# A three-stage decoder on one core: masks and maxima per head on VectorE, heads added from PSUM, layernorm's step on ScalarE, new plan costs

## The chip, the core and the metric

The kernel runs on one core of one Trainium2 chip. A core has TensorE (PE) for matrix products, VectorE (DVE), ScalarE (ACT), GpSimd (POOL), and SyncE (SP), which issues the DMAs. Each engine takes its instructions in order from its own queue; engines wait for each other by semaphores. TensorE writes its results to PSUM, of which this kernel uses eight banks of 128 x 512 float32[...]. The metric is the device time in microseconds of one execution.

## What is computed

There are 32 batch entries of 128 tokens with 128 features, in float32. Three stages follow each other, each with a residual sum and a layernorm:

```python
x = layernorm(x + attn(x, W))               # 16 heads of width 8, q = k = y; values are the whole x
x = layernorm(x + xattn(x, ctx, ctx, ...))  # 16 heads of width 8, band mask |i-j| <= 64
x = layernorm(x + ffn(x, ...))              # two layers, below
```

In the first stage each head's output is `attn @ x` (128 x 128), and the 16 heads are joined by one weight matrix of 2048 x 128. A layer of the third stage is

```python
h = shift_token(x); q, k, v = split(h @ wqkv)          # 8 heads of width 64
q = l2norm(q) * qs; k = l2norm(k) * ksc; q, k = rotary_xpos(q, k)
sim = (8 * q) @ k.T; sim[(i < j) | (i > j + 64)] = -max; x = x + (softmax(sim) @ v) @ wo
h = layernorm(shift_token(x)) * lg + lb; a, g = split(h @ w1 + b1)
x = x + (a * gelu(g)) @ w2 + b2
```

## The kernel before

**Order of the work.** The 32 entries are cut into ten groups (SIZES, one to four entries). A list of generator steps, sorted by due times made from LAGS, CLOSE and SPREAD, interleaves four stages of different groups: self_attention, cross_attention, and layer 0 and layer 1. The steps do not issue instructions; they record operations in a `Plan`, each with an engine, a cost in ns, the values it reads and writes, and flags. `Plan.issue` then simulates the five engines with these costs and fixes the order on each engine: it takes the operation that can start first, among those at most AHEAD operations beyond the first undone one. The same step hands out buffers from rings, PSUM banks (`m`, eight), large SBUF tiles (`big`) and small ones, some of which (KEEP) are held back for the oldest value that waits. So costs and constants decide the order of instructions, and with it who waits for whom.

**Self attention** (`self_half`, one call for each half of eight heads of an entry, 64 calls). TensorE makes x W_h for four heads at a time (L579, 128x512), which ScalarE copies to `zs` (L586). Scores come from a split into bf16 parts (L542). VectorE takes the maxima of each bank of four heads (L421, in `maxima`), GpSimd splits them in two bf16 parts (L435, L436), TensorE turns them and subtracts them in PSUM (L442, L452), and ScalarE takes exponentials of a whole bank (L600). TensorE multiplies by `zs`, which has a column of ones for the sums (L608), into three banks of three, three and two heads. VectorE takes reciprocals (L617) and multiplies a whole bank into `zs` (L618). GpSimd adds the eight heads in three steps, 4, 2 and 1 wide (L628), and adds the result to the residual `x0` (L632).

**Cross attention** (`cross_batch`, 32 calls of two halves). The band mask is a matmul of an identity with a bf16 mask, 128x512, into each bank (L539), and the scores accumulate on it. VectorE takes the maxima, ScalarE one exponential per head with the negated maximum as bias (L466, in `exps_of`), TensorE turns the result (L481, in `turned_half`), VectorE copies it (L488) and TensorE multiplies by the values (L724).

**Local attention** (`local_batch`, 64 calls). TensorE makes q, k and v (L796) and ScalarE copies them (L801). ScalarE squares q and k (L807), VectorE sums the squares (L810), GpSimd raises the sums to the power -1/2 (L813, L814). The rotary step is a product with the swapped halves on GpSimd (L824) and three VectorE steps over q and k together, 128x1024: product with the cosines (L833), sum (L837), product with the norms (L840). Eight transposes (L851) and copies (L857), then scores of 64-row matmuls on top of the mask matmuls (L865, L871), maxima and exponentials with row sums (L421, L466), division (L885, L886), transposes, output and projection (L900, L912), residual (L919).

**Layernorm** (`layernorm`): statistics on VectorE (L382, L389), the power on GpSimd (L397 to L400), and scale and shift by one VectorE instruction per entry (L407).

VectorE and GpSimd steps marked `port=True` are booked as sharing a port.

Of the kernel before, what the change touches and what calls it, by code (L numbers as in the profile page):

```python
# [28 lines left out]
AHEAD = 430  # L29
LAGS = (0, 1.35, 2.75, 4.1)  # L30
RINGS = (23, 16, 6, 4)
KEEP = (2, 3, 5)
NEAR = 0
EARLY = (0, 0.2)
CLOSE = (0.9, 0.85, 0.9, 1, 1, 1, 1.2, 1.05, 0.85, 0.95)
SPREAD = (1.4, 1.0, 0.7, 1.5)
LH, LD = 8, 64
INNER = LH * LD
# [38 lines left out]
class Plan:  # L77

# [51 lines left out]
    def issue(self, ahead, near=80.0, hop=60.0, table_ns=1300.0, tiling_ns=160.0, dma_ns=1800.0):  # L132
# [13 lines left out]
        def time_of(k):  # L146
            e = ops[k][0]
            return max([0.0] + [end[d] + (hop if ops[d][0] != e else 0.0) for d in ops[k][3]])
# [5 lines left out]
        shared = 0.0  # L154
# [5 lines left out]
        while len(order) < n:  # L160
            best = None
            for e in engines:
                choice, least = [], None
                for k, t in ready[e]:
                    if k > first + ahead:
                        continue
                    start = max(clock[e], t, shared if ops[k][7] else 0.0)
# [5 lines left out]
                    for vs in need.values():  # L173
# [4 lines left out]
                        start = max(start, sorted(q.free)[len(vs) - 1][0] + hop)  # L178
# [4 lines left out]
                    if e == "PE" and ops[k][8][0] != state:  # L183
                        start += tiling_ns
# [19 lines left out]
            if e == "SP":  # L204
                line = max(line, s + dma_ns) + ns
                end[k], clock[e] = line + 400.0, s + 450.0
            else:
                end[k] = clock[e] = s + ns
            if tab:
                table[e] = tab  # L210
            if port:
                shared = end[k]
# [19 lines left out]
def decoder_kernel(ctx: ExitStack, tc: tile.TileContext, a: dict, out: bass.AP):  # L232
# [109 lines left out]
    def prepare_cross():  # L342
# [3 lines left out]
               cols[:, 0:1], cols[:, 0:1], SCALE, 1.0, ALU.mult, ALU.mult), [], [w_cross])  # L346
# [15 lines left out]
    def turned(src, n):  # L362

        tp, t = Val(mring), Val(mid)
        op("PE", 113 * n, turn(src, tp, n), [src], [tp], hold=[t])
        op("ACT", 140 + 113 * n,
# [10 lines left out]
    def layernorm(src, dst, n):  # L377
# [6 lines left out]
        op("DVE", n * 290, stats, [src], [st])  # L384
# [6 lines left out]
        op("DVE", n * 175, aggr, [st], [mv])  # L391
# [10 lines left out]
        op("POOL", 1100 + 260 * n, rest, [], [mv])  # L402

        def apply():
            x, y = group(src.t), group(dst.t)
            for j in range(n):
                nc.vector.tensor_scalar(  # L407
                    y[:, j, :], x[:, j, :], mv.t[:, 8 + j : 9 + j], mv.t[:, 12 + j : 13 + j],
                    ALU.mult, ALU.add,
                )  # L410

        op("DVE", 200 * n, apply, [mv] + ([src] if src is not dst else []), [dst])
# [4 lines left out]
    def maxima(s, nm):  # L417
        for b in range(2):
            op(
                "DVE", 690,  # L420
# [5 lines left out]
    def minus_max(s):  # L426
# [6 lines left out]
        def parts():  # L433
# [4 lines left out]
        op("POOL", 440, parts, [nm], [hl])  # L438
        mp = Val(mring, lambda t: t[:, 0:64].bitcast(BF16))
        op(  # L440
            "PE", 110,
# [4 lines left out]
        op("ACT", 260, lambda: nc.scalar.copy(mT.t, mp.t), [mp], [mT])  # L446
        return mT

    def emit_max(s, mT):
        for b in range(2):  # L450
            for i in range(4):
# [3 lines left out]
                )  # L455

    def exps_of(s, sums=None):
# [4 lines left out]
        for b in range(2):  # L462
# [8 lines left out]
            op("ACT", 4 * (345 if sums else 255) + 60, exps, [s[b], (nm, b)],  # L471
# [3 lines left out]
    def turned_half(e, et, b, eng, src):  # L475
# [9 lines left out]
        op("PE", 4 * 113, pe, [src], [tp], hold=[et])  # L485
        copy = nc.vector.tensor_copy if eng == "DVE" else nc.scalar.copy
        op(eng, 690 if eng == "DVE" else 590,
# [6 lines left out]
    def in_slots(src, n, keep_src, moving):  # L494
# [4 lines left out]
        op("ACT", 140 + 113 * n,  # L499
           lambda: nc.scalar.copy(pv.t[:, 0, every], src.t[:, every]), [src], [(pv, 0)])  # L500
        op("POOL", 316 * n,
# [3 lines left out]
        op("ACT", 140 + 113 * n,  # L505
           lambda: nc.scalar.copy(pv.t[:, 1, every], rest.t[:, every]), [rest], [(pv, 1)])
        op("POOL", 316 * n,
# [26 lines left out]
    def scores_of(s, stationary, moving, hh, window=False):  # L534
# [12 lines left out]
        op("PE", 8 * 62 + 432 * window, pe,  # L547
# [22 lines left out]
    def self_half(j, hh, x0, xT, ys):  # L570
# [3 lines left out]
        for b in range(2):  # L574
# [3 lines left out]
                "PE", 875,  # L578
# [6 lines left out]
                "ACT", 590,  # L585
# [10 lines left out]
        op("PE", 8 * 60, lambda: emit_max(s, mT), [mT, (w_self, 2)], s)  # L596
        e = Val(big, heads)
        for b in range(2):
            op("ACT", 590,
# [3 lines left out]
        for k, (h0, n) in enumerate(((0, 3), (3, 3), (6, 2))):  # L603
# [9 lines left out]
            op("PE", 230 * n, pe, [e] + [(zs, i) for i in range(3)], [oz])  # L613
            rl = Val(small)

            def scale(oz=oz, rl=rl, h0=h0, n=n):
                nc.vector.reciprocal(rl.t[:, 0:n], oz.t[:, 0:n, D])  # L617
                nc.vector.tensor_tensor(  # L618
                    zs.t[:, h0 : h0 + n, 0:D], oz.t[:, 0:n, 0:D],
                    rl.t[:, 0:n].unsqueeze(2).to_broadcast([P, n, D]), ALU.mult,  # L620
                )

            op("DVE", 175 + 30 + 133 * n, scale, [oz], [rl, (zs, ("o", k))])

        z = lambda h0, n: zs.t[:, h0 : h0 + n, 0:D]
        for n, ns in ((4, 1270), (2, 730), (1, 450)):
            op("POOL", ns,
# [495 lines left out]
```

## Time and profile before

Three runs took 1293.61, 1292.23 and 1289.26 us; the median is 1292.23. The profiled execution took 1292.12 us, with a span of 1290.3 us between its first and last instruction and a granted TensorE clock of 0.987.

| Line | Engine, operation | Count | Busy us |
|---|---|---|---|
| L466 | ACT exponentials of the masked stages | 1024 | 323.0, and 115.9 for 512 accumulator reads |
| L421 | DVE maxima | 384 | 245.6 |
| L813 | POOL power | 64 | 200.8 |
| L628, L632 | POOL additions of heads | 256 | 163.2 and 31.8 |
| L618, L617 | DVE scaling of heads, reciprocals | 192, 192 | 98.7, 32.4 |
| L833, L840, L837 | DVE rotary and norms | 64 each | 86.0, 87.2, 80.5 |
| L407 | DVE layernorm's step | 160 | 72.3 |
| L539, L865 | PE mask matmuls | 128, 128 | 48.7, 39.1 |

How to read the profile: the page has busy time of each engine, the span in 40 equal slices with the busy share in tenths, the chain of work that ended last (followed back from the last instruction to what released each step), and groups of instructions by line with their busy time, the mean length of one, and the idle time of the engine before them with what ended it. `big<-m,sm` names the tiles written and read, without buffer numbers. The timeline lists instructions by start. Busy time is a union: where an instruction begins before its predecessor's recorded end, the overlap counts once. Ends of matmuls are modelled.

### The profile page before, as it was taken

What the parts mean: (1) busy time and instruction counts of PE and PEld (TensorE: products, weight loads), DVE (VectorE), ACT (ScalarE), POOL (GpSimd) and SP (SyncE); (2) the same over time, 40 slices, a digit from 0 to 9 for tenths busy, and PEclk for the clock granted to TensorE, in tenths of its full rate; (3) what the DMA queues carried; (4) which work ended last, traced back from release to release, by engine and by line L of the source; (5) the groups of instructions that cost most, each with busy time, mean ns of one, the idle gap of its engine ahead of it and who ended that gap; (6) DMA issues with size and microseconds to landing.
All of it is one profiled execution on the core that took longest, in us unless ns stands there. A gap on an engine that the chain in (4) does not pass through costs nothing.

```text
span 1290.3 us, 27579 instructions
## 1 busy us (share of the span) xinstructions
PE 1213.9 (94%) x9730; PEld 888.0 (69%) x9730; DVE 1070.3 (83%) x2134; ACT 966.2 (75%) x2762; POOL 835.3 (65%) x1094
## 2 busy tenths in 40 slices
PE   7988999999979999999999999999999989999996
PEld 4766677776767865777777667778667657567664
DVE  2677889878968888887798889979899999988786
ACT  4564777777867778777778778858889968879863
POOL 2866657765857389555687468653966963786454
PEclk9999999999989999999999999999999989999999
DMA  9886414240154420732005401330300000000000
GB/s 254 209 213 193 124 39 105 56 128 9 37 136 109 99 56 1 174 89 65 20 25 138 124 1 34 94 95 18 97 2 12 18 18 2 9 1 2 2 1 25
DMA packets 173930, 91.44 MB, mean 71 GB/s; under 512 B 155872, under 2 KB 161888, under 8 KB 173536
## 3 DMA queue, kind: packets, MB, share of 16 engines
q1 hardware_dynamic: 173792, 89.67, 27.5%
q8 instruction: 77, 1.26, 0.4%
q14 instruction: 61, 0.50, 0.1%
HBM read 49.79 MB, written 39.85 MB: 69 GB/s over the span
## 4 chain that ended last, share of the span: by engine, by line
PE 45%; POOL 15%; DVE 14%; ACT 6%; issue 3%; DMA 1%; SPq 0%; POOLq 0%; DVEq 0%; ACTq 0%
PE m L796 6%; POOL sm L813 6%; PE m L481 5%; PE m L944 4%; PE m L608 4%; ACT big L466 3%; PE m L900 3%; PE m L579 3%; PE m L871 3%; PE m L912 3%; POOL big L824 3%; PE m L964 3%; PE m L724 2%; DVE sm L421 2%; PE m L542 2%
## 5 line engine op out<-in xcount | busy, mean ns | idle before, releaser
L466 ACT ACTIVATE big<-m,sm 128x128 f32<-128x128 f32 x1024 | 323.0, 399 | 54.5 <-DVE sm L421 53.9
L421 DVE TENSOR_REDUCE sm<-m 128x4 f32<-128x512 f32 x384 | 245.6, 681 | 45.4 <-PE m L871 21.5
L813 POOL TENSOR_TENSOR sm<-sm,nhalf 128x16 f32<-128x16 f32 x64 | 200.8, 3137 | 36.8 <-DVE sm L810 26.7
L628 POOL TENSOR_TENSOR big<-big 128x512 f32<-128x512 f32 (+2 forms) x192 | 163.2, 850 | 83.8 <-DVE big L618 36.8
L824 POOL TENSOR_TENSOR big<-big,layer_w 128x512 f32<-128x512 f32 x128 | 162.4, 1269 | 76.4 <-ACT big L801 71.1
L796 PE MATMUL m<-layer_w,mid 128*128 128x512 f32 x384 | 193.2, 612 | 4.2 <-DVE xb L971 2.1
L481 PE MATMUL m<-ident,big 128*128 128x128 f32 x1024 | 144.4, 276 | 15.4 <-DVE big L886 9.6
L481 PEld LDWEIGHTS m<-ident,big 128*128 128x128 f32 x1024 | 115.7, 141 | 54.9 <-issue 21.9
L579 PE MATMUL m<-self_w,mid 128*128 128x512 f32 x256 | 131.1, 626 | 7.0 <-DMA self_w<-in_self_w 5.7
L608 PEld LDWEIGHTS m<-big,big 128*128 128x128 f32 x1024 | 123.0, 191 | 13.7 <-issue 7.5
L608 PE MATMUL m<-big,big 128*128 128x129 f32 x1024 | 129.9, 276 | 0.9 <-DVE big L618 0.3
L466 ACT ACTIVATION_READ_ACCUMULATOR big<-m,sm 128x1 f32 x512 | 115.9, 226 | 0.0
L586 ACT COPY big<-m 128x512 f32<-128x512 f32 x128 | 75.1, 600 | 38.8 <-PE m L579 38.0
L618 DVE TENSOR_TENSOR big<-m,sm 128x384 f32<-128x384 f32 (+1 forms) x192 | 98.6, 514 | 6.6
L886 DVE TENSOR_TENSOR big<-big,sm 128x512 f32<-128x512 f32 x128 | 98.2, 767 | 4.6 <-DMA slots<-big 0.2
L542 PEld LDWEIGHTS <-big 72*128 72x128 bf16 x1024 | 72.3, 98 | 41.3 <-issue 20.2
L542 PE MATMUL m<-big,big 72*128 72x128 bf16 x1024 | 87.8, 220 | 9.6 <-DMA big<-slots 8.9
L488 ACT COPY big<-m 128x512 f32<-128x512 f32 x128 | 75.0, 598 | 28.3 <-PE m L481 19.4
L796 PEld LDWEIGHTS m<-layer_w,mid 128*128 128x128 f32 x384 | 64.7, 193 | 42.6 <-issue 27.9
L857 ACT COPY big<-m 128x512 f32<-128x512 f32 x128 | 71.6, 608 | 29.7 <-PE m L851 29.1
L944 PE MATMUL m<-mid,layer_w 128*128 128x512 f32 (+7 forms) x240 | 89.5, 516 | 2.7 <-DVE mid L935 1.5
L488 DVE COPY big<-m 128x512 f32<-128x512 f32 x128 | 82.0, 681 | 11.5 <-PE m L481 10.7
(116 smaller groups left out, 2611.4 us busy)
## 6 DMA issues: line engine op xcount, KB each, us to landing
slots<-big SPq DMA_DIRECT2D x384, 96.0 KB
big<-slots SPq DMA_DIRECT2D x128, 288.0 KB
layer_w<-in_layer_w SPq DMA_DIRECT2D x2, 1877.0 KB
mid<-in_xt SPq DMA_DIRECT2D x5, 256.0 KB
mid<-in_xg SPq DMA_DIRECT2D x5, 256.0 KB
mid<-in_ct SPq DMA_DIRECT2D x5, 256.0 KB
out<-xb SPq DMA_DIRECT2D x5, 256.0 KB
self_w<-in_self_w SPq DMA_DIRECT2D x2, 512.0 KB
```

The lines of the kernel that those rows point to most:

```text
L421: lambda b=b: nc.vector.tensor_reduce(nm.t[:, 4 * b : 4 * b + 4], s[b].t, AX.X, ALU.max, negate=True),
L466: nc.scalar.activation(e.t[:, h, :], s[b].t[:, h - 4 * b, :], AF.Exp, bias=nm.t[:, h : h + 1], accum_out=sums.t[:, h : h + 1] if sums else ...
L481: nc.tensor.transpose(tp.t[:, 128 * c : 128 * c + 128], e.t[:, 4 * b + c, :], ident)
L488: lambda: copy(et.t[:, 4 * b : 4 * b + 4, :], tp.t.rearrange("p (c k) -> p c k", c=4)),
L542: nc.tensor.matmul(s[b].t[:, i, :], st[:, h, :], mv[:, h, :], start=not window and i == 0, stop=i == 3,)
L579: lambda zp=zp, h0=h0: nc.tensor.matmul(zp.t, group(xT.t)[:, j, :], attn_w[:, h0 : h0 + 4, :], start=True, stop=True),
L608: nc.tensor.matmul(oz.t[:, i, :], e.t[:, h0 + i, :], zs.t[:, h0 + i, :], start=True, stop=True,)
L628: lambda n=n: nc.gpsimd.tensor_tensor(z(0, n), z(0, n), z(n, n), ALU.add),
L796: lambda hp=hp, i=i: nc.tensor.matmul(hp.t, group(hT.t)[:, j, :], wqkv[l][:, INNER * i : INNER * (i + 1)], start=True, stop=True),
L813: nc.gpsimd.tensor_tensor(rn.t[:, 0:16], rn.t[:, 0:16], nhalf, ALU.pow)
L824: nc.gpsimd.tensor_tensor(r2.t[:, :, :, d0 : d0 + 32], q[:, :, :, d1 : d1 + 32], tabs[l][:, :, d0 : d0 + 32].unsqueeze(2).to_broadcast([P, ...
L944: lambda t=t, off=off, c0=c0, m=m: nc.tensor.matmul(t.t[:m, every], w1[l][:, off + c0 : off + c0 + m], hT.t[:, every], start=True, stop=True),
```

## The change

1. The heads of self attention are no longer written back to `zs` and added by GpSimd. After the reciprocals, VectorE runs one scalar-tensor-tensor instruction per head: x0's entry = PSUM head times its reciprocal, plus x0's entry. L618, L628 and L632 go.
2. The band masks are no longer matmuls. The tables maskw and maskl are negated, and q (through SCALE and the rotary tables) is negated too, so that the scores arrive negated. One VectorE instruction per head adds the mask, multiplies by a scale, writes the masked negated score to SBUF, and gives its minimum as an accumulator output. The exponential then reads SBUF, in place, with scale -1.
3. In local attention that scale is q's norm, per row and head, so q's own norm step goes. The cosine products read PSUM directly, q and k apart, and the sums and k's norm are 128x512 steps. The transposes of q can begin when q's part is there.
4. Layernorm's step moves to ScalarE, one activation per entry with scale and bias.
5. The plan: all costs of operations are new, an engine's tail and hop times replace one hop time, the port's booking is per engine, and AHEAD, LAGS, RINGS, KEEP, NEAR, CLOSE and SPREAD have new values.

The diff, cut to its core (the changed costs of untouched operations are left out):

```diff
-AHEAD = 430
-LAGS = (0, 1.35, 2.75, 4.1)
-RINGS = (23, 16, 6, 4)
-KEEP = (2, 3, 5)
-NEAR = 0
+AHEAD = 290
+LAGS = (0, 1.55, 2.75, 4.1)
+RINGS = (23, 17, 6, 4)
+KEEP = (2, 2, 5)
+NEAR = 60
...
-CLOSE = (0.9, 0.85, 0.9, 1, 1, 1, 1.2, 1.05, 0.85, 0.95)
-SPREAD = (1.4, 1.0, 0.7, 1.5)
+CLOSE = (0.9, 0.85, 0.9, 1, 1, 1, 1.15, 0.95, 0.85, 0.95)
+SPREAD = (1.3, 1.0, 0.7, 1.5)
...
+TTR = 215
...
+    TAIL = {"PE": 165.0, "DVE": 82.0, "ACT": 115.0, "POOL": -75.0, "SP": 0.0}
+    HOP = {"PE": 55.0, "DVE": 32.0, "ACT": 36.0, "POOL": 77.0, "SP": 25.0}
...
-                nc.vector.tensor_scalar(
-                    y[:, j, :], x[:, j, :], mv.t[:, 8 + j : 9 + j], mv.t[:, 12 + j : 13 + j],
-                    ALU.mult, ALU.add,
+                nc.scalar.activation(
+                    y[:, j, :], x[:, j, :], AF.Identity,
+                    scale=mv.t[:, 8 + j : 9 + j], bias=mv.t[:, 12 + j : 13 + j],
                 )
-        op("DVE", 200 * n, apply, [mv] + ([src] if src is not dst else []), [dst])
+        op("ACT", 365 * n, apply, [mv] + ([src] if src is not dst else []), [dst])
...
+    def masked_exps(s, mask, scale=lambda h: 1.0, sums=None, extra=()):
+        nm = Val(small)
+        e = Val(big, heads)
+        for b in range(2):
+            def masked(b=b):
+                for h in range(4 * b, 4 * b + 4):
+                    nc.vector.tensor_tensor_reduce(
+                        out=e.t[:, h, :], in0=s[b].t[:, h - 4 * b, :], in1=mask,
+                        scale=scale(h), scalar=-MASKED, op0=ALU.add, op1=ALU.min,
+                        accum_out=nm.t[:, h : h + 1],
+                    )
+            op("DVE", TTR * 4, masked, [s[b], (w_self, 2), *extra], [(e, b), (nm, b)])
+            def exps(b=b):
+                for h in range(4 * b, 4 * b + 4):
+                    nc.scalar.activation(
+                        e.t[:, h, :], e.t[:, h, :], AF.Exp, bias=nm.t[:, h : h + 1], scale=-1.0,
+                        accum_out=sums.t[:, h : h + 1] if sums else None,
+                    )
+            op("ACT", 1384 if sums else 1004, exps, [(nm, b)],
+               [(e, b)] + ([(sums, b)] if sums else []), table="exp")
+        return e
...
             def scale(oz=oz, rl=rl, n=n):
+                y = group(x0.t)[:, j, :]
                 nc.vector.reciprocal(rl.t[:, 0:n], oz.t[:, 0:n, D])
-                nc.vector.tensor_tensor(
-                    zs.t[:, h0 : h0 + n, 0:D], oz.t[:, 0:n, 0:D],
-                    rl.t[:, 0:n].unsqueeze(2).to_broadcast([P, n, D]), ALU.mult,
-                )
+                for i in range(n):
+                    nc.vector.scalar_tensor_tensor(
+                        y, oz.t[:, i, 0:D], rl.t[:, i : i + 1], y, ALU.mult, ALU.add
+                    )
-        z = lambda h0, n: zs.t[:, h0 : h0 + n, 0:D]
-        for n, ns in ((4, 1270), (2, 730), (1, 450)):
-            op("POOL", ns,
-               lambda n=n: nc.gpsimd.tensor_tensor(z(0, n), z(0, n), z(n, n), ALU.add),
-               [], [zs], port=n > 1)
-        y = lambda: group(x0.t)[:, j, :]
-        op("POOL", 450,
-           lambda: nc.gpsimd.tensor_tensor(y(), y(), z(0, 1)[:, 0, :], ALU.add),
-           [zs], [(x0, j)])
+            op("DVE", 100 + 205 * n, scale, [oz], [rl, (x0, j)])
...
-            scores_of(s, qs, ks, hh, True)
-            e = exps_of(s)
+            scores_of(s, qs, ks, hh)
+            e = masked_exps(s, maskw[:, 0:P])
...
+            if i < 2:
+                op("DVE", 620,
+                   lambda hp=hp, i=i: nc.vector.tensor_tensor(
+                       qr.t[:, i], hp.t.rearrange("p (h d) -> p h d", d=LD),
+                       tabc[l][:, i].unsqueeze(1).to_broadcast([P, LH, LD]), ALU.mult),
+                   [hp, w_layer[l]], [(qr, i)])
...
+        for i in range(2):
+            op("DVE", 610,
+               lambda i=i: nc.vector.tensor_tensor(qr.t[:, i], qr.t[:, i], r2.t[:, i], ALU.add),
+               [r2], [(qr, i)], port=True)
+        op("POOL", 3171, power, [], [rn])
+        op("DVE", 610,
+           lambda: nc.vector.tensor_tensor(
+               qr.t[:, 1], qr.t[:, 1],
+               rn.t[:, 8:16].unsqueeze(2).to_broadcast([P, LH, LD]), ALU.mult),
+           [rn], [(qr, 1)], port=True)
...
-            for b in range(2):
-                nc.tensor.matmul(
-                    s[b].t, identb, maskl, start=True, stop=False
-                )
...
-        e = exps_of(s, rl)
+        norm = lambda h: rn.t[:, 2 * (h % 4) + h // 4 : 2 * (h % 4) + h // 4 + 1]
+        e = masked_exps(s, maskl[:, 0:P], norm, rl, [rn])
```

## The prediction

> **What bounds the kernel now.** I read the page first: busy time by engine, the slices, the chain that ended last.
>
> ```profile
> PE 1213.9 (94%) x9730; PEld 888.0 (69%) x9730; DVE 1070.3 (83%) x2134; ACT 966.2 (75%) x2762; POOL 835.3 (65%) x1094
> ...
> PE   7988999999979999999999999999999989999996
> ...
> DVE  2677889878968888887798889979899999988786
> ACT  4564777777867778777778778858889968879863
> POOL 2866657765857389555687468653966963786454
> ...
> PE 45%; POOL 15%; DVE 14%; ACT 6%; issue 3%; DMA 1%; SPq 0%; POOLq 0%; DVEq 0%; ACTq 0%
> ```
>
> TensorE is full in nearly every slice; the chain stays longest on it. Busy time over stretches of the span confirms it for the long middle (columns PE, PEld, DVE, ACT, POOL):
>
> ```profile
> 0.00:35.00 35.00, 27.42 (x118) 15.00 (x119) 9.88 (x22) 17.79 (x34) 7.92 (x39) 1.00 0.92 262
> ...
> 130.00:1150.00 1020.00, 978.44 (x7961) 719.74 (x7959) 878.93 (x1718) 795.64 (x2295) 683.86 (x831) 0.99 0.25 61
> ```
>
> In the middle TensorE fills 978.4 of 1020 us, 96%, beside a VectorE at 86%. VectorE is thus second, with about 10% to spare. In the first 35 us it has hardly any work (9.9 us): its first reduction starts at 26.5 us.
>
> Then the groups by shape, for the price of each edited line (busy us, mean ns of one):
>
> ```profile
> L421 DVE TENSOR_REDUCE sm<-m 128x4 f32<-128x512 f32 x384 | 245.6, 681 | 45.4 <-PE m L871 21.5 <-PE m L542 18.3 <-ACT big L600 4.2
> ...
> L618 DVE TENSOR_TENSOR big<-m,sm 128x384 f32<-128x384 f32 x128 | 71.5, 558 | 4.4
> ...
> L539 PE MATMUL m<-masks,identb 128*128 128x512 bf16 x128 | 48.7, 381 | 1.2 <-DVE big L618 1.1
> ...
> L407 DVE TENSOR_SCALAR mid<-mid,sm 128x128 f32<-128x128 f32 x64 | 31.4, 546 | 8.2 <-POOL sm L400 8.2
> ...
> L389 DVE BATCH_NORM_AGGREGATE sm<-sm 128x2 f32<-128x6 f32 x160 | 15.9, 155 | 0.2
> ```
>
> A mean duration is not what an instruction costs its queue, so last the timeline (start, length, instruction, how many merged):
>
> ```profile
> 607.95 1.87 DVE L421 TENSOR_REDUCE sm<-m 128x4 f32<-128x512 f32 x3
> ...
> 622.80 0.17 DVE L617 RECIPROCAL sm<-m 128x3 f32<-128x3 f32 x1
> 623.01 0.56 DVE L618 TENSOR_TENSOR big<-m,sm 128x384 f32<-128x384 f32 x1
> ...
> 1282.45 0.57 DVE L954 SCALAR_TENSOR_TENSOR mid<-m,cross_w,mid 128x128 f32<-128x128 f32 x2
> ```
> ```profile
> 658.99 0.59 PE L865 MATMUL m<-masks,identb 128*128 128x512 bf16 x2
> 659.51 0.72 PE L871 MATMUL m<-big 64*128 64x128 f32 x8
> ```
>
> Three independent reductions take 1.87 us: (1.87-0.68)/2 = 0.60 us apart though each lasts 0.68. So an independent successor starts 0.08 us before the end. A dependent one does not: L618 needs L617's result and starts 0.21 us after a 0.17 us start, 0.03 us behind its end. These two prices, "duration less 0.08" and "duration plus 0.03", carry my sum.
>
> **The change, part by part.**
>
> *TensorE.* The 256 mask matmuls go (L539, L865). Their durations (48.7 + 39.1 us) overlap the next matmul: two of L865 hold the queue from 658.99 to 659.51, 0.26 us each, and L539 costs about 0.59-0.38 = 0.21. 128 x 0.21 + 128 x 0.26 = 60 us off. TensorE: 1213.9 - 60 = 1154. This is on the path today.
>
> *VectorE, maxima.* 256 of the 384 reductions go: 245.6 x 2/3 = -164 us. In their place come 1024 one-head instructions (128x128, PSUM and mask to SBUF), each with an accumulator output. The built order of the changed kernel shows 2048 instructions at that line, as the Trainium skill says of an op that writes its accumulator ("VectorE: DVE Perf Modes", "Two Vector instructions with no wait between them": the main one and an accumulator read). The trace has no such VectorE pair. For the main one the nearest rows are the two-input PSUM ones: 128x128 of L919, 288 ns, less 0.08 = 0.21; and in the local layers, where q's norm is a per-partition operand, L954 at 128x128, 336 ns, less 0.08 = 0.26 (the x2 row: 0.57-0.34 = 0.23). For the read the nearest is another tiny output, L389: three in 0.30 us, 0.07 us each. Sum 512 x (0.21+0.07) + 512 x (0.26+0.07) = 312 us. The read's ends are 0.015 us (the plan's own 215 ns a head) and its full 0.155: -56 to +87 us. I take 0.07, which is an independent row of that size. Here a rule speaks against the change: the same page, "The DRAIN you can't avoid", has the next op wait until the pipeline is empty (it exempts ops that are not held). Read strictly, each would cost its whole duration, 512 x (0.29+0.155) + 512 x (0.34+0.155) = 481 us, 170 us more, and the kernel would end far above 1400. The three reductions in 1.87 us say otherwise, so the row decides.
>
> *VectorE, heads.* L618 goes: 71.5 + 27.2 = -99 us (the reciprocals stay). 512 scalar-tensor-tensor steps come, all into the same 128 columns of x0: in the built order every one waits for the one before. A link costs 0.34+0.03 = 0.37 us, the last of a group of three or two 0.26: 320 x 0.37 + 192 x 0.26 = +168 us. The plan books 205 ns each, 105 us; without the waits it would be 512 x 0.26 = 133. I take 168. Queued behind each wait is all of VectorE's work, and TensorE's next bank: the bank is held 0.20 + 2 x 0.37 + 0.26 = 1.2 us instead of 0.20+0.48.
>
> *VectorE, the rest.* Layernorm's step leaves (L407, four forms: 31.4+15.3+14.6+11.0 = -72 us, a third of it waiting for GpSimd, since the median one lasts 0.34 us). The rotary lines L833, L837, L840 (86.0+80.5+87.2 = 254 us) become 128 products from PSUM at 0.60 (L971's 0.685 less 0.08), 128 sums at 1.258/2+0.04 = 0.67, and 64 norms of k at 1.362/2+0.04 = 0.72: 77+86+46 = 209, so -45 us. VectorE: 1070.3 - 164 + 312 - 99 + 168 - 72 - 45 = 1170 us. That is 100 more, and more than TensorE's 1154.
>
> *ScalarE.* +160 layernorm steps of 0.25 to 0.37 us (128x128 of L950 lasts 0.366): +40 to +59. The 1024 exponentials now read SBUF: the SBUF cast at L500 lasts 636 ns where the PSUM copy L586 lasts 600: 1024 x 0.036 = +37 (ends 0 and 60). About 1055 us, 83% of the new span, hidden. If VectorE and TensorE were both quick, it would be the next limit.
>
> *GpSimd.* L628 and L632 go: 163.2 + 31.8 = -195 us. Cover it had, so nothing directly; 15% of the chain lay on it, above all the power (L813) and rotary steps near 1000-1050 us, and those stay.
>
> *Waits, order, DMA.* The local maxima now need q's power from GpSimd. The norm of k, queued nearby, waits for the same result, as L840 does today: no price. A score bank is freed after about 1.2 us of VectorE instead of a reduction and four exponentials: a gain for TensorE, zero while it isn't the bound. The count of DMAs stays 384, 128 and 30. The plan's new constants reorder everything; no row prices that, and I take zero, with 1% (13 us) to each side.
>
> **The sum.** VectorE becomes the bound: 26.5 us before its first reduction, 3 us after its last step, between them 1170 us at some filling. TensorE reaches 96% in the middle today, with a free VectorE beside it; VectorE would have TensorE at 91% and ScalarE at 83% beside it. I take 94.5%: 1170/0.945 = 1238, + 29.5 = 1268 span. The profiled execution took 1292.12 us with a span of 1290.3, 1.8 more, and the median of the runs is 1292.23, so the two agree: 1270 us, 1.7% less.
>
> **Rivals.**
> 1. *VectorE is cheap, TensorE stays the bound.* If a head costs the plan's 215 ns in the one-head instructions (220 us, not 312) and 205 ns in the chain (105, not 168), VectorE is 1170 - 92 - 63 = 1015. TensorE's 1154 at today's 94% is 1228 + 2 = 1230 us. For: the new plan books just these; against: they lie under the rows of the trace (0.26 for one L954).
> 2. *Slower: VectorE's queue doesn't fill.* The mechanism is the bank held by the chained steps. Eight PSUM banks serve all; scores, heads and transposes all wait behind 1.2 us blocks of VectorE, TensorE stalls on banks, and then VectorE starves in turn. At 91% filling: 1170/0.91 + 29.5 + 1.8 = 1317 us. It decides from a filling under 1170/(1292-31) = 92.8%. For: the chain is booked at half its price in the plan, so the order is wrong for it; three engines are close to full. Against: VectorE already stands at 9 in six slices in a row, the 30th to the 35th.
> 3. *ScalarE with its table loads and exponentials* becomes a co-bound in the local layers: 1055 + 60 at 88% = 1267, not distinguishable in time; it shows as VectorE idle behind ScalarE.
>
> That the change does not do what it says is excluded by the built order: 256 matmuls and 256 GpSimd additions are gone.
>
> **Chances.** Forecast 0.45 (0.33 faster, 0.08 same, 0.04 slower), rival 1 0.18, rival 2 0.29 (0.02 of it same), rival 3 0.08 (0.04 faster, 0.04 slower). Faster by over 0.3% (about 4 us, what a measurement can tell from no change) 0.55, same 0.10, slower 0.35. The range 1220 to 1318 takes in rival 1 and most of rival 2; the forecast alone would be 1245 to 1296 (filling 96.5% to 92.5%).
>
> **What would show it.** Right: VectorE's share at 91-93% and above TensorE's; the head steps about 0.37 us apart, the one-head instructions with reads 0.28 to 0.33 us per head. Wrong: pairs at 0.22 us or chains at 0.20 (rival 1: TensorE stays at 94%); VectorE under 90% with idle time ended by TensorE (rival 2). A pair above 0.4 us would put the time beyond the range.

## The result, and the profile after

The changed kernel takes 1381.0 us (median of four runs, 1377.35 to 1386.05), the kernel before 1292.58 us on the same chip. The ratio is 1.069, with an interval of 1.065 to 1.073: slower by 88 us, where 22 us less were forecast. The profiled execution took 1377.35 us with a span of 1375.6.

The page of the changed kernel: busy time, four rows of slices, and the chain that ended last.

```profile
PE 1209.3 (88%) x9474; PEld 894.1 (65%) x9474; DVE 1132.4 (82%) x4214; ACT 1052.0 (76%) x2918; POOL 585.9 (43%) x838
...
PE   8889988989989888889988988898888999979886
...
DVE  3778998887996999688886888879978988898864
ACT  5456767868887877687876967887887989798975
...
PEclk9899999999999999999999999999998999999898
...
PE 28%; DVE 19%; ACT 11%; issue 3%; DMA 1%; POOL 1%; SPq 0%; DVEq 0%; POOLq 0%; ACTq 0%
```

No engine is full now. TensorE fell from 94% to 88%, and VectorE stayed at about 82% though it has 62 us more to do. The chain's shares are of the span, and the chain could be followed over only 63% of it (84% before), so they are read against each other: TensorE holds 28 of these 63, VectorE 19 and ScalarE 11; before, TensorE held 45 of 84, VectorE 14 and ScalarE 6. The same stretch of the middle as before (columns PE, PEld, DVE, ACT, POOL, granted clock):

```profile
130.00:1150.00 1020.00, 909.11 (x7338) 676.03 (x7336) 874.95 (x3348) 804.19 (x2259) 431.33 (x589) 0.96 0.25 64
```

In the same 1020 us TensorE is busy 69 us less than before (978.44), and VectorE 4 us less (878.93): the engine that was to become the bound gets no further in that time than when it was the second.

The groups of the new instructions (busy us, mean ns of one, idle time ahead):

```profile
L487 ACT ACTIVATE big<-big,sm 128x128 f32<-128x128 f32 x1024 | 356.0, 394 | 21.4 <-DVE sm L477 17.9 <-DMA big<-slots 2.9
L660 DVE SCALAR_TENSOR_TENSOR mid<-m,sm,mid 128x128 f32<-128x128 f32 x512 | 179.7, 351 | 18.2
L477 DVE CUSTOM_DVE_ANT_0 big<-m,masks,sm 128x128 f32<-128x128 f32 x512 | 143.8, 346 | 11.6 <-PE m L902 11.2
L477 DVE CUSTOM_DVE_ANT_0 big<-m,masks 128x128 f32<-128x128 f32 x512 | 113.2, 285 | 4.8 <-PE m L581 3.8 <-issue 0.5 <-ACT big L892 0.5
...
L477 DVE DVE_READ_ACCUMULATOR2_ANT sm<- 128x1 f32 x1024 | 84.7, 83 | 0.1
...
L418 ACT ACTIVATE mid<-mid,sm 128x128 f32<-128x128 f32 x64 | 26.8, 487 | 4.7 <-POOL sm L411 4.6
```

And VectorE's timeline (start, length):

```profile
606.10 0.08 DVE L477 DVE_READ_ACCUMULATOR2_ANT sm<- 128x1 f32 x1
606.10 0.28 DVE L477 CUSTOM_DVE_ANT_0 big<-m,masks 128x128 f32<-128x128 f32 x1
606.31 0.08 DVE L477 DVE_READ_ACCUMULATOR2_ANT sm<- 128x1 f32 x1
606.31 0.28 DVE L477 CUSTOM_DVE_ANT_0 big<-m,masks 128x128 f32<-128x128 f32 x1
...
607.78 1.12 DVE L660 SCALAR_TENSOR_TENSOR mid<-m,sm,mid 128x128 f32<-128x128 f32 x3
...
618.99 0.34 DVE L477 CUSTOM_DVE_ANT_0 big<-m,masks,sm 128x128 f32<-128x128 f32 x1
...
619.26 0.34 DVE L477 CUSTOM_DVE_ANT_0 big<-m,masks,sm 128x128 f32<-128x128 f32 x1
```

The one-head instructions start 0.21 us apart in cross attention and 0.27 us apart in local attention; the accumulator's read begins with the next instruction and costs nothing. Three chained head steps take 1.12 us, that is (1.12-0.35)/2 = 0.385 us a link. So the one-head instructions cost less than was forecast, and a link of the chain a little more (0.385 us for 0.37).

What TensorE waits for has changed. The two largest waits at the transposes of the exponentials (L520; us in all, number of waits, the longest), and below them the first of the two in the kernel before, where the lines were L481 and L466:

```profile
PEld m L520 <- ACT big L487: 58.9, 53, 7.1
...
PE m L520 <- DVE big L919: 22.2, 23, 3.1
```
```profile
PEld m L481 <- ACT big L466: 6.3, 12, 1.2
```

### The profile page after: what moved, and what is told of

The parts are those of the page before. It is cut to its first block, busy times and chain, and to the rows that moved or that the text cites. A ratio compares the mean times of both kernels' runs of the same rounds, so it can differ in the third digit from the quotient of the medians.

```text
span 1375.6 us, 29062 instructions
## 1 busy us (share of the span) xinstructions
PE 1209.3 (88%) x9474; PEld 894.1 (65%) x9474; DVE 1132.4 (82%) x4214; ACT 1052.0 (76%) x2918; POOL 585.9 (43%) x838
## 4 chain that ended last, share of the span: by engine, by line
PE 28%; DVE 19%; ACT 11%; issue 3%; DMA 1%; POOL 1%; SPq 0%; DVEq 0%; POOLq 0%; ACTq 0%
DVE big L477 7%; ACT big L487 5%; PE m L829 4%; PE m L520 4%; PE m L977 3%; DVE mid L660 3%; PE m L933 3%; DVE big L919 2%; PE m L618 2%; PE m L945 2%; PE m L997 2%; PE m L886 2%; PE m L647 1%; DVE big L871 1%; PE m L581 1%
## 5 line engine op out<-in xcount | busy, mean ns | idle before, releaser
L487 ACT ACTIVATE big<-big,sm 128x128 f32<-128x128 f32 x1024 | 356.0, 394 | 21.4 <-DVE sm L477 17.9
L520 PE MATMUL m<-ident,big 128*128 128x128 f32 x1024 | 159.2, 294 | 69.2 <-DVE big L919 22.2
L520 PEld LDWEIGHTS m<-ident,big 128*128 128x128 f32 x1024 | 123.7, 150 | 117.3 <-ACT big L487 58.9
L862 POOL TENSOR_TENSOR big<-big,layer_w 128x512 f32<-128x512 f32 x128 | 144.1, 1126 | 120.5 <-ACT big L834 84.9
L660 DVE SCALAR_TENSOR_TENSOR mid<-m,sm,mid 128x128 f32<-128x128 f32 x512 | 179.7, 351 | 18.2
L477 DVE CUSTOM_DVE_ANT_0 big<-m,masks,sm 128x128 f32<-128x128 f32 x512 | 143.8, 346 | 11.6 <-PE m L902 11.2
L618 PE MATMUL m<-self_w,mid 128*128 128x512 f32 x256 | 131.5, 633 | 9.6 <-DMA self_w<-in_self_w 5.5
L477 DVE CUSTOM_DVE_ANT_0 big<-m,masks 128x128 f32<-128x128 f32 x512 | 113.2, 285 | 4.8 <-PE m L581 3.8
L892 ACT COPY big<-m 128x512 f32<-128x512 f32 x128 | 72.7, 594 | 41.4 <-PE m L886 40.4
L834 ACT COPY big<-m 128x512 f32<-128x512 f32 x128 | 73.2, 592 | 39.9 <-PE m L829 24.6
L487 ACT ACTIVATION_READ_ACCUMULATOR big<-big,sm 128x1 f32 x512 | 99.4, 194 | 0.0
L625 ACT COPY big<-m 128x512 f32<-128x512 f32 x128 | 73.1, 590 | 31.3 <-PE m L618 30.6
L840 DVE TENSOR_TENSOR big<-m,layer_w 128x512 f32<-128x512 f32 x128 | 85.1, 683 | 13.9 <-PE m L829 7.3
L527 ACT COPY big<-m 128x512 f32<-128x512 f32 x128 | 73.2, 585 | 30.5 <-PE m L520 29.4
L432 DVE TENSOR_REDUCE sm<-m 128x4 f32<-128x512 f32 x128 | 81.8, 682 | 16.0 <-PE m L581 14.9
```

Source lines behind the costliest of these rows:

```text
L477: nc.vector.tensor_tensor_reduce(out=e.t[:, h, :], in0=s[b].t[:, h - 4 * b, :], in1=mask, scale=scale(h), scalar=-MASKED, op0=ALU.add, op1 ...
L487: nc.scalar.activation(e.t[:, h, :], e.t[:, h, :], AF.Exp, bias=nm.t[:, h : h + 1], scale=-1.0, accum_out=sums.t[:, h : h + 1] if sums els ...
L520: nc.tensor.transpose(tp.t[:, 128 * c : 128 * c + 128], e.t[:, 4 * b + c, :], ident)
L618: lambda zp=zp, h0=h0: nc.tensor.matmul(zp.t, group(xT.t)[:, j, :], attn_w[:, h0 : h0 + 4, :], start=True, stop=True),
L660: nc.vector.scalar_tensor_tensor(y, oz.t[:, i, 0:D], rl.t[:, i : i + 1], y, ALU.mult, ALU.add)
L840: lambda hp=hp, i=i: nc.vector.tensor_tensor(qr.t[:, i], hp.t.rearrange("p (h d) -> p h d", d=LD), tabc[l][:, i].unsqueeze(1).to_broadcast ...
```

## The experiments

After the result six theories stood side by side. (A) The chain of head steps is booked at 205 ns and lasts 385, so the plan's order is wrong for it. (B) The heads' steps themselves are too dear for VectorE. (C) The plan and its constants are to blame. (D) The exponentials are mispriced. (E) The way from scores to transposes has become longer (VectorE, then ScalarE from SBUF), and TensorE idles behind it. (F) Layernorm's step blocks ScalarE. Later came (O): the order as such, drawn anew by any change of a cost, carries a few per cent. All ratios are to the kernel before on the same chip; its medians there lay between 1288.9 and 1292.6 us, so a difference between two kernels that didn't run side by side is good to some 4 us.

**One part undone, or another price**

*Heads at their measured price.*

```diff
-            op("DVE", 100 + 205 * n, scale, [oz], [rl, (x0, j)])
+            op("DVE", 86 + 385 * n, scale, [oz], [rl, (x0, j)])
```

> The changed kernel with one number changed: a group of n heads is booked in the plan at 86 + 385 n ns, which is what its reciprocal and chained steps took in the profile after, instead of 100 + 205 n. Same instructions, another order. Theory A (the order is wrong because the plan books the chain at half its price): TensorE's idle falls back from 152 us towards 60 and the time to about 1300 us. Theory B (the chain itself, its 385 ns a link and the banks it holds, is what costs): about 1370 us, less than 1% from the changed kernel.

Measured 1375.1 us (1.065 [1.061, 1.070]), 6 us under the changed kernel. The wrong price is not the cause; A falls.

*Heads as before* (one product into `zs`, sums on GpSimd).

```diff
-                    nc.vector.scalar_tensor_tensor(
-                        y, oz.t[:, i, 0:D], rl.t[:, i : i + 1], y, ALU.mult, ALU.add
-                    )
+                nc.vector.tensor_tensor(
+                    zs.t[:, h0 : h0 + n, 0:D], oz.t[:, 0:n, 0:D],
+                    rl.t[:, 0:n].unsqueeze(2).to_broadcast([P, n, D]), ALU.mult,
+                )
```

> The changed kernel with the heads added as before: VectorE scales a whole bank into zs, GpSimd adds in four steps; booked at the measured turns. Masks, q's norm, layernorm on ScalarE and the new plan stay. VectorE loses 512 x 0.34 = 175 us and gets 99 back. Theory A and theory B both: well under the changed kernel, near 1250 us (TensorE 1137 us of queue time at 0.92, plus what GpSimd does). Theory C (the new plan itself, its constants and costs, makes the idle time, whatever VectorE does): stays above 1330 us.

Measured 1360.6 us (1.055 [1.050, 1.061]). Without the heads' new steps, and with an order of its own, the kernel is 20 us shorter; three quarters of the loss are still there.

*The old constants with the new steps* (AHEAD 430, LAGS, RINGS, KEEP, NEAR, CLOSE and SPREAD as before).

```diff
-AHEAD = 290
+AHEAD = 430
...
-NEAR = 60
+NEAR = 0
```

> The changed kernel with the eight plan constants of the kernel before (AHEAD, LAGS, RINGS, KEEP, NEAR, CLOSE, SPREAD), all else as changed. Theory C, constants: under 1330 us. Theories A and B: within 2% of the changed kernel, 1355 to 1405 us, since the order still counts on a chain that is half as long.

Measured 1418.2 us (1.099 [1.094, 1.105]), 37 us more than with the new constants. They are not the cause.

*The plan alone* (its costs, tails, hops and constants, and the split rotary step; heads, masks, q's norm and layernorm as before).

```diff
-            e = masked_exps(s, maskw[:, 0:P])
+            e = exps_of(s)
...
-        op("ACT", 365 * n, apply, [mv] + ([src] if src is not dst else []), [dst])
+        op("DVE", 257 * n, apply, [mv] + ([src] if src is not dst else []), [dst])
```

> Only the plan of the change (new costs, tails, hops, constants); heads, masks, q's norm and layernorm as before, booked at measured turns. The rotary products stay split into q and k from PSUM. Theory C: over 1320 us, most of the loss is there without the new instructions. Theories A and B: 1290 us or less, within 2% of the kernel before.

Measured 1318.7 us (1.022 [1.018, 1.027]), with the granted clock at 0.988, as before. The plan with nearly the old work costs 29 us (1289.8 on that chip): less than C expected, more than A and B did.

*All new steps at their measured prices.*

```diff
-            op("DVE", TTR * 4, masked, [s[b], (w_self, 2), *extra], [(e, b), (nm, b)])
+            op("DVE", 1080 if extra else 840, masked, [s[b], (w_self, 2), *extra], [(e, b), (nm, b)])
...
-            op("ACT", 1384 if sums else 1004, exps, [(nm, b)],
+            op("ACT", 1550 if sums else 1170, exps, [(nm, b)],
```

> The changed kernel with the plan's costs of the new steps at what the profile after shows: heads 86 + 385 n, four masked minima 840 (cross) and 1080 (local), four exponentials from SBUF 1170 and with sums 1550, layernorm's step 389 n. Same instructions. Theory D (the transposes wait 59 us for exponentials that the plan books 170 ns too short per four): the wait of L520 for L487 falls under 20 us and the time to 1320 us or less. Theory E (the chain from scores to transposes is longer, minima then exponentials, whatever is booked): above 1360 us.

Measured 1413.3 us (1.094 [1.089, 1.099]). Truer prices made it 32 us slower, with not one instruction changed, and the wait for the exponentials that D would cut under 20 us stands at 62.4. D falls.

*Layernorm's step back on VectorE.*

```diff
-                nc.scalar.activation(
+                nc.vector.tensor_scalar(
```

> The changed kernel with layernorm's step on VectorE again (booked 257 n). Theory F (each step holds ScalarE's queue behind GpSimd's power, and all exponentials with it): 1340 us or less. Theory E: within 1.5% of 1381, since layernorm is rare beside the masked stages.

Measured 1398.4 us (1.082 [1.077, 1.087]), 17 us more than with it on ScalarE, though the transposes wait less for the exponentials (35.8 us instead of 58.9). F's gain of 40 us isn't there.

*Masks as before* (mask matmuls, bank maxima, exponentials from PSUM, q's own norm).

```diff
-            scores_of(s, qs, ks, hh)
-            e = masked_exps(s, maskw[:, 0:P])
+            scores_of(s, qs, ks, hh, True)
+            e = exps_of(s)
```

> The changed kernel with mask matmuls, bank-wide maxima, exponentials from PSUM and q's norm as before (rotary still split from PSUM, q's norm a step of its own, booked 610). TensorE gets its 60 us back. Theory E: faster than the changed kernel in spite of that, 1330 to 1345 us (the plan alone took 1319, plus about 20 for the heads), with a granted clock back at 0.98. Theory D or F alone: 1400 us or more.

Measured 1357.7 us (1.051 [1.046, 1.056]). With about 60 us more work for TensorE the kernel is 23 us shorter, and the clock is 0.977. The sign is E's, but the time lies above the 1330 to 1345 us that E expected, and the order was drawn anew here too.

*The new steps under the old plan* (old constants and hop, new steps at measured prices).

```diff
-            e = exps_of(s, rl)
+            e = masked_exps(s, maskl[:, 0:P], norm, rl, [rn])
...
-        op("DVE", 200 * n, apply, [mv] + ([src] if src is not dst else []), [dst])
+        op("ACT", 400 * n + 80, apply, [mv] + ([src] if src is not dst else []), [dst])
```

> The kernel before with the four new kinds of steps, but the old plan: its constants, its single hop, its old costs (durations rather than turns), the new steps booked at their measured durations. Theory C (most of the loss is the new plan): under 1310 us. Theories D and E: 1340 us or more, since the plan alone took only 29 us.

Measured 1438.7 us (1.114 [1.108, 1.122]). The plan and the steps don't add up: 29 us for the plan, 146 us for the steps under the old plan, 88 for both, and each of the three has an order of its own.

**How far an order alone reaches**

*Two controls: AHEAD moved by 10.*

```diff
-AHEAD = 430
+AHEAD = 420
```

> Control: the kernel before with AHEAD 420 instead of 430 and nothing else. No instruction is added or removed, only the order that the plan makes is another. If the time hangs on the work and the waits named so far, it stays within 1% of 1292 us (1280 to 1305). If the order itself, as drawn from tuned constants, carries a few per cent (theory O), it comes out 2 to 6% slower (1318 to 1370), and part of the loss of the change needs no cause but that its order was drawn anew.

```diff
-AHEAD = 290
+AHEAD = 300
```

> Control: the changed kernel with AHEAD 300 instead of 290 and nothing else; only the order is another. Theory O expects anything from 1340 to 1440 us. If orders count for little, 1368 to 1390. The distance from 1381 is the size below which differences between kernels whose plans differ mean nothing.

Measured 1304.5 us (1.012 [1.008, 1.016]) and 1387.0 us (1.076 [1.073, 1.080]). Both lie at the upper edge of what was expected if orders count for little: a new order costs 14 and 6 us here, and the last run will show 45 for another. So a gap of 20 us between kernels with different orders, as for the heads or the masks, can't be put down to the instructions.

**Work added or taken at a fixed order.** In the next six kernels the bookings stay, so every other instruction keeps its place on its engine.

*No chain*: the head steps write apart, and the heads' sum is left out.

```diff
-                        y, oz.t[:, i, 0:D], rl.t[:, i : i + 1], y, ALU.mult, ALU.add
+                        zs.t[:, h0 + i, 0:D], oz.t[:, i, 0:D], rl.t[:, i : i + 1], y,
+                        ALU.mult, ALU.add
```

> The changed kernel, same order on every engine, but each head's scalar-tensor-tensor step writes to a place of its own instead of the sum: no link waits for the one before, and the heads' sum is left out of the computation. VectorE saves 320 links x (0.385-0.267) = 38 us. If the blocks of chained steps starve TensorE (rival 2 of the prediction), 1381 falls by more than 38 us, to 1300 to 1340. If VectorE is a plain bound at this point, by 38 to about 1343. If what is lost lies in other waits, by less than half of it: 1362 to 1380.

The page and the timeline of this kernel:

```profile
PE 1201.3 (89%) x9474; PEld 892.6 (66%) x9474; DVE 1103.2 (82%) x4214; ACT 1051.7 (78%) x2918; POOL 585.7 (43%) x838
```
```profile
623.28 0.87 DVE L660 SCALAR_TENSOR_TENSOR big<-m,sm,mid 128x128 f32<-128x128 f32 x3
```

Three steps now take 0.87 us, 0.26 us apart. The time is 1342.4 us (1.041 [1.037, 1.046]): 38.6 us less than the changed kernel (36 by the ratios), for 42 us less in VectorE's queue. The queue is counted in the trace: each stretch of VectorE without a gap over 0.06 us, from its first start to its last end, less the 0.08 us by which an independent successor would have started earlier; it fell from 1138 to 1096. VectorE's idle time, span less busy, is 1346.5-1103.2 = 243 us in the profiled execution, as in the changed kernel (1375.6-1132.4 = 243). Thus the time of the chain goes into the span nearly one to one, though VectorE idles for 18% of it. Shortening a block of three steps from 1.12 to 0.87 us gives back the steps' own time and no more.

*TensorE filler*: one more matmul ahead of each four transposes, in the changed kernel and in the kernel before.

```diff
         def pe():
+            nc.tensor.matmul(tp.t, identb, maskl, start=True, stop=True)
             for c in range(4):
```

> The changed kernel, same order, with one more matmul (identity by mask, 128x512, its result overwritten) ahead of each four transposes of the exponentials (L520), the place where TensorE waits most: 256 x 0.23 = 59 us more work for TensorE, in part in time in which it waits anyway. If TensorE's idle time, and the halved clock after it, is what is lost, the granted clock rises from 0.956 towards 0.98 and the time stays at 1365 to 1395 us. If TensorE is a bound, 1420 to 1440 us. If the slow clock has nothing to do with its idle gaps, the granted clock stays at 0.95 to 0.96.

> The kernel before, same order, with one more matmul (identity by mask, 128x512, overwritten) ahead of each four transposes (L481): 256 x 0.23 = 59 us more for TensorE. If TensorE alone is the bound of before, as the prediction had it, 1290 rises by 50 to 60 to about 1345. If before is bound by several engines in alternation, by a part of it: 1300 to 1325.

Measured 1393.7 us (1.081 [1.077, 1.085]) and 1317.1 us (1.021 [1.019, 1.023]). In the trace each filler takes 0.22 us of the queue, 256 of them 56 us; of these, 13 us come through in the changed kernel (0.23 for each us) and 28 in the kernel before (0.50). So TensorE alone was not the bound even before. In the changed kernel the clock rose from 0.956 to 0.968, which is worth some 17 us of full-speed time and may be part of why so little came through.

*VectorE filler in the kernel before*: a copy behind each maxima step.

```diff
                     nm.t[:, 4 * b : 4 * b + 4], s[b].t, AX.X, ALU.max, negate=True),
+                    nc.vector.tensor_copy(scr, ident)),
```

> The kernel before, same order, with one more VectorE instruction (a copy of 128x128 in SBUF, its result not used) behind each maxima step (L421): 384 x about 0.17 = 65 us more for VectorE, whose idle time was 220 us. If VectorE's idle time is spare room, as the prediction took it to be, the time stays within 15 us: 1290 to 1305. If VectorE's time goes into the span though it is idle for 17% of it, 1325 to 1355; then the 60 us that VectorE gains by the change explain most of the loss.

Measured 1341.9 us (1.041 [1.037, 1.044]). VectorE's group for the filler:

```profile
L424 DVE COPY scr<-ident 128x128 f32<-128x128 f32 x384 | 140.4, 366 | 0.0
```

The copies lengthen VectorE's queue by 103 us (counted in the same way, from 1062 to 1165); 53 us come through, 0.51 for each us. About half of the 103 us is time in which a copy was held by GpSimd (last section), so this is the price of VectorE being held, whatever holds it. Of the 220 us in which VectorE was idle before the change, these copies could use about 50.

*ScalarE filler*: a copy behind each four exponentials, in both kernels.

```diff
                         accum_out=sums.t[:, h : h + 1] if sums else None,
                     )
+                nc.scalar.copy(scr, ident)
```

> The changed kernel, same order, with one more ScalarE instruction (a copy of 128x128 in SBUF, its result not used) behind each four exponentials (L487): 256 x about 0.27 = 70 us more for ScalarE. If ScalarE has become a co-bound (rival 3 of the prediction), 1381 rises by 50 us or more, to 1430 to 1460. If its 24% of idle time is room, 1381 to 1400.

> The same ScalarE filler in the kernel before (behind each four exponentials of L466): 256 x about 0.27 = 70 us more. If ScalarE's idle time is room there, 1290 to 1310. If every engine's time goes in part into the span, 1320 to 1350; the difference to the changed kernel's rise tells whether the change moved ScalarE nearer to the path.

Measured 1401.1 us (1.086 [1.084, 1.088]) and 1303.5 us (1.011 [1.008, 1.015]): of 49 us of filler 20 come through after the change (0.41), of 50 us 14.5 before it (0.29).

**One part of the change alone, and the same part with a new order**

*Layernorm's step on ScalarE in the kernel before, booked as before.*

```diff
-                nc.vector.tensor_scalar(
-                    y[:, j, :], x[:, j, :], mv.t[:, 8 + j : 9 + j], mv.t[:, 12 + j : 13 + j],
-                    ALU.mult, ALU.add,
+                nc.scalar.activation(
+                    y[:, j, :], x[:, j, :], AF.Identity,
+                    scale=mv.t[:, 8 + j : 9 + j], bias=mv.t[:, 12 + j : 13 + j],
                 )
```

> The kernel before with layernorm's step on ScalarE alone (part 4 of the change), its booking left on VectorE, so that all other instructions stay in their order on every engine. VectorE loses 72 us, ScalarE gains 160 x about 0.37 = 59 us. By the slopes 0.51 and 0.29: -37 + 17 = -20, so 1290 becomes 1270 (1262 to 1280), below both kernels. If VectorE's idle time is spare room (the prediction's view), only ScalarE's 17 us count: 1295 to 1310. If slopes hold for added work only, 1285 to 1295.

*The same instructions, booked on ScalarE.*

```diff
-        op("DVE", 200 * n, apply, [mv] + ([src] if src is not dst else []), [dst])
+        op("ACT", 389 * n, apply, [mv] + ([src] if src is not dst else []), [dst])
```

> The same move with layernorm's step booked on ScalarE (389 ns each), so that the plan draws the order anew with the old constants. If a redrawn order costs about 1% by itself, as AHEAD 420 did (+14 us), 1280 to 1295. If orders are drawn equally well, the same as n1_ln_in_place within 8 us. If the old constants fit only the old costs, above 1310.

The busy rows of the two, in this order:

```profile
PE 1217.1 (94%) x9730; PEld 889.4 (69%) x9730; DVE 1010.0 (78%) x1974; ACT 1023.8 (79%) x2922; POOL 839.6 (65%) x1094
```
```profile
PE 1237.7 (92%) x9730; PEld 899.3 (67%) x9730; DVE 1006.4 (75%) x1974; ACT 1021.3 (76%) x2920; POOL 829.8 (62%) x1094
```

Measured 1297.5 us (1.0045 [1.0028, 1.0061]) and 1342.5 us (1.040 [1.038, 1.042]). Two things follow. The slopes missed the first by 26 us: 60 us less on VectorE and 58 more on ScalarE gained nothing, and VectorE's idle time grew from 220 to 285 us. If ScalarE's 58 us cost 0.29 each, 17 us, then VectorE's 60 gave back 11, a third of what 0.51 would give. That is an estimate, since no run takes work off VectorE in the kernel before without putting it elsewhere. And the second has the same matmuls and VectorE instructions, and but for two fewer on ScalarE the same in all; its booking drew another order, and that alone costs 45 us, 3.5%. No version tried beat the kernel before.

## Why the prediction was wrong

**Most terms of the sum held.** VectorE's queue was put at 1170 us; in the trace it is about 1138. The accumulator reads cost 0 and not 0.07 us each: the 1024 one-head instructions take 512 x 0.21 + 512 x 0.27 = 246 us, not 312. (The plan's 215 ns were right for cross attention.) Part of these 66 us was made up by an error the other way: the sum takes old instructions off at their durations and puts new ones on at their turns, 0.08 us less each. By turns, the reductions and L618 free some 25 us less. The chain is 0.385 us a link where 0.37 was taken. Layernorm's VectorE rows are gone. The rotary step gave less for the same reason: L840, L871 and L875 have durations of 222 us against 254, -32 and not -45. ScalarE was put at 1055 and is busy 1052, by some luck: exponentials +33 us for the +37 forecast, layernorm's step 67 us of busy time, above the 40 to 59, and 16 us less for the accumulator reads of ScalarE (115.9 to 99.4), which the sum didn't have. GpSimd lost its 256 additions. The mask matmuls were put at 60 us; 256 fillers of the same kind take 56.

**The step that failed is "I take 94.5%: 1170/0.945 = 1238".** It takes the fullest engine's work and divides by a filling that TensorE had before. With VectorE's true work of 1132 us the span would have been shorter still, 1132/0.945 + 29.5 = 1227; it was 1375.6. The forecast left VectorE 1268-1170 = 98 us of idle time. It idles for 243 us, even a little more than the 220 before. The fixed-order runs show why such a step can't be made here: none of the engines was *the* bound. Before the change an added us of TensorE, VectorE or ScalarE cost 0.50, 0.51 and 0.29 us, so VectorE "with about 10% to spare" was already wrong of the kernel before, where it stood at 83%, and ScalarE's 1055 us were not "hidden". After the change they cost 0.23, (taken away) 0.92 and 0.41: VectorE did move onto the path, as forecast, but as one of several engines that wait for each other in turn, not as a queue that fills. GpSimd was given no filler, so what its 250 us less are worth is not known.

**The second failed step is "The plan's new constants reorder everything; no row prices that, and I take zero, with 1% (13 us) to each side".** The size was wrong by up to four times. The same instructions as in the changed kernel (from two fewer to four more on ScalarE) ran in six orders:

| Same work as the changed kernel | Median us |
|---|---|
| heads booked at their price | 1375.1 |
| the changed kernel | 1381.0 |
| AHEAD 300 | 1387.0 |
| all steps booked at their price | 1413.3 |
| the old constants | 1418.2 |
| the old plan | 1438.7 |

From the first to the last it is 64 us, 4.6%. Truer prices don't have to give shorter times. The order of the kernel before is a good draw for its instructions: a step of 10 in AHEAD costs it 14 us, a new booking of one step 45.

**The rivals.** Rival 2 had the sign, and the right sight of it (VectorE under 90%, idle behind others), but the runs don't show its mechanism: without the chain the time falls by the chain's own 38.6 us, not by more, so the longer hold of the bank stalls nobody beyond that. (The bank is still held for 0.87 us of head steps there.) Rival 3 is there in part (ScalarE's 0.41). Rival 1's price for the one-head instructions was the nearer one, 220 us where 246 were measured and 312 forecast, and still the time went the other way.

**Where the 88 us are.** VectorE's queue grew by 76 us, ScalarE's by about 90 (counted in the same way, with 0.12 us for the 0.08), TensorE lost about 60. With the slopes of before and after, that is an estimated 39 to 70, 26 to 37, and -30 to -14 us: 35 to 93 in all. The plan alone is 29 us more. That covers the loss, but it is an estimate and no proof: the slopes failed for moved work in the layernorm run, and each undone part is read through an order of its own. How much belongs to the work and how much to the order stays open; a search for a better order of the new instructions was not tried, and only that could tell. Shown is that the chain costs 38.6 us at a fixed order, and that no tried order of the new work comes below 1375. Undoing the masks gives 23 us back and undoing the heads 20, but a redrawn order alone moved the time by 6 to 45 us in other runs, so neither is shown to be a cost of the instructions.

**The clock.** The granted clock fell from 0.987 to 0.956; in full-speed time that is 0.044 x 1375.6 = 60 us lost, against 17 before, and the trace has it at half in 22 pieces (7 before), 12 of 3.4 us, 7 of 6.8, 2 of 10.2, and a last one of 13.4 that runs past the end. The Trainium skill ("TensorE: Matmul & The Clock Gate", Part 1) says that the rate is halved after an idle window of about 3.4 us and comes back after as long a busy one, so by the page the waits would be paid twice, an estimated 60-17 = 43 us. The lengths agree. That the window must be idle does not: in the 3.4 us ahead of 21 of the 22 pieces TensorE was busy for 14% to 74% of the time, with no gap over 2.6 us; only one followed an idle stretch. So short waits that leave TensorE half busy came before the half rate too. But the clock doesn't decide the time: with AHEAD 300 it is 0.970, worth 19 us, and that kernel is 6 us slower; with layernorm undone 0.966 and 17 us slower. The masks' 23 us go with a better clock (0.977), but no run separates the two.

## What to carry to other kernels

When three engines stand between 75 and 94%, don't divide the fullest one's work by a hoped-for filling: add a known filler to each engine at a fixed order and read how much of it comes through, since an idle 17% may in large part be waiting that no work can use. Work moved off such an engine may give back less than it costs on the other. And where a planner fixes the order, first measure how far the time moves when only the order is redrawn (here 0.4% to 4.2%); an edit that changes a booked cost is judged against that.

## What the runs showed of the hardware

- A VectorE accumulator output costs no time of its own: the read (83 ns recorded) runs beside the next one-head instruction, 0.21 us apart with a constant scale and 0.27 with a per-partition one.
- A VectorE copy from SBUF to SBUF is held up by some GpSimd work. Of the 384 filler copies, 107 had no GpSimd instruction beside their first 0.21 us and took 216 ns on average, 227 at most; the other 277 took 423 ns on average, up to 1230. Behind a rotary product or an addition of heads that was under way on GpSimd, the copy ended 0.08 us after the GpSimd instruction did, in each of the 76 such copies that began with 0.15 us or more of it still to go. Beside GpSimd's power step (3.07 us) they took 215 ns, and ended up to 2.6 us before it:

```profile
602.91 0.21 DVE L424 COPY scr<-ident 128x128 f32<-128x128 f32 x1
603.04 0.68 DVE L422 TENSOR_REDUCE sm<-m 128x4 f32<-128x512 f32 x1
```

  These two rows of the filler kernel show a free copy: the next instruction starts 0.13 us after it. The 277 longer ones took 277 x (0.423-0.216) = 57 us more than free ones would have, about half of the filler's 103 us.
- ScalarE's exponential of 128x128 starts its successor after 0.29 us from SBUF (in place), 0.25 from PSUM, and with a sum read in between after 0.385 and 0.343: 0.042 us more each, 43 us for 1024. The busy time of the group grew by 33.
